# Where sixteen tiles of a rotated context are prepared: twelve in layer 0's attention, four in its feed-forward, none in layer 1's cross attention

## The chip, the cores and the metric

The kernel runs on one core of a Trainium2 chip. The core has five engines that run side by side, each with its own instruction stream: TensorE (PE, matrix products and transposes through them), VectorE (DVE), ScalarE (ACT), GpSimd (POOL) and SyncE (SP, which issues DMA transfers here). They wait for each other through semaphores. The metric is the device time of one execution in microseconds; lower is better.

## The reference

The model is a two-layer perceiver. A latent array `x` of 64 batches with 32 rows of 256 attends to a context `ctx_512` of 64 batches with 257 rows of 64. Each layer is a cross attention, a self attention and a feed-forward, each on a layer norm of `x` and added to `x`:

```python
x = x + _L0_xattn_ref(_layernorm(x), ctx_512, ...)
x = x + _L0_attn_ref(_layernorm(x), ...)      # 16 heads of 128, l2-normed queries and one key head
x = x + _L0_ffn_ref(_layernorm(x), ...)       # 16 blocks of 64; each row uses its 4 likeliest blocks
x = x + _L1_xattn_ref(_layernorm(x), ctx_512, ...)
x = x + _L1_attn_ref(_layernorm(x), ...)      # causal
x = x + _L1_ffn_ref(_layernorm(x), ...)       # 8 experts, one per row
```

The part that matters is the context of layer 1's cross attention, which is rotated by position (rope):

```python
kv_rope = kv_c * cos[None] + _rotate_half(kv_c) * sin[None]
q_r = jnp.einsum('bshq,hqr->bhsr', q_big, W_qr)
k_r = jnp.einsum('bld,hdr->bhlr', kv_rope, W_kr)
attn = jax.nn.softmax(jnp.einsum('bhsr,bhlr->bhsl', q_r, k_r), axis=-1)
ctx_c = jnp.einsum('bhsl,bld->bhsd', attn, kv_rope)
```

`kv_rope` depends on the inputs only, so it can be computed at any time before layer 1. And the feed-forward of layer 0, beside which part of it is now computed:

```python
prob = softmax(xf @ Wr.T + br); _, idx = top_k(prob, 4)      # mask[n, block] = 1 for the four
h = gelu(einsum('nf,ibf->nib', xf, W1b)) * mask[:, :, None]
y = einsum('nib,fib->nf', h, W2b)
```

## The kernel before

The 2048 latent rows are 16 tiles of 128 rows (`NT = 16`), in 4 groups of 4 tiles (`NG = 4`). A context tile `t` is the context of four batches. The stages follow each other in time:

- A (0 to about 130 us): layer 0's cross attention.
- B (130 to 505): layer 0's self attention as a row of slots, one tile entering at each slot `t`. It also holds group 0 of the feed-forward and the block choices of the first groups in its late slots. The order on PE, DVE, ACT and POOL is the order in which the code is written.
- C (505 to 640): groups 1, 2 and 3 of the feed-forward, and small products that fold layer 1's weights (`chain_1`, `chain_2`, `chain_m`, `chain_n`). Only PE's and ACT's order is the written one; a scheduler orders DVE, POOL and SP by its own model of the work.
- D (640 to 990): layer 1's cross attention, 64 blocks `b`, four to a context tile. Then layer 1's self attention and the experts.

**Fetch and rotate.** `fetch(t, work)` (L688) issues ten DMAs on SP: for each half of the tile, the transposed context into `rct` and its two halves swapped into `rrt`; and four pieces of the untransposed context into `rna`. `rotate(t, work)` (L701) runs seven POOL operations on them (two multiplies and an add for the transposed copy, four for the other, L705 to L715), and issues two stores to `ctd` and one to `nad` in DRAM. The tiles `rct`, `rrt`, `rna` and `rnt` have one buffer each, so a fetch waits until the rotation and the stores before it are done with it. Before the change, `rotate(t // 2)` stands at the even slots 0 to 14 of B (tiles 0 to 7) and eight more in D at `b` = 2, 6, ..., 30. Stage D loads `ctd` and `nad` tile by tile.

**The feed-forward.** For each group `g`, `hidden(g, f, ...)` makes eight pieces `hc{g}_{f}` of the hidden layer (matmuls L639, gelu on ACT L646) and multiplies each with its mask `mb[f]` on DVE (L647). The mask of a group is made by `choose_blocks` and `choose_best` (L571 to L615, small DVE operations on 128 x 64 logits: `lgc`, `mxc`, `eqc`, `m2c`, `onec`, `maskc`), written to DRAM as `maskd` (L625) and spread over the partitions by 16 loads (L631, `spread`). `output(g, hs, i, ...)` (L649) then sums the eight pieces for tile `i` into PSUM (`yc`, L652) and adds them to `x` (L659). PE runs, for each `g`, the eight hidden pieces, the choice's logits (`lpc`, for g = 2), the first chains, four outputs with turns between, and the second chains:

```python
chains = {
    (1, 1): [lambda z=z, c=c: chain_1(z, c) for z in range(2) for c in range(2)],
    (2, 0): [lambda z=z: chain_2(z) for z in range(2)],
    (2, 1): [lambda z=z, k=k: chain_m(z, k) for k in range(KC) for z in range(2)],
    (3, 0): [lambda r=r: chain_n(r) for r in range(4)],
}
```

`chain_1` (L1048) multiplies `d_rt` with `d_kr` into `t1`; `chain_2` (L1061) makes `t2` (`d_t2`) out of `t1` and `d_at`; both are copied from PSUM by DVE (L1055, L1068). The weights `d_q`, `d_at`, `d_wo`, `d_kr`, `d_rt`, `d_c` are loaded on SP's queue at the head of C (L1023 to L1035).

**In B**, the steps that the prediction names are: the squares of the queries on POOL (`q2b`, L789), the norm of the projected output (`lnb_bo`, `ynb`), the products with the values (`avb`, L848) and the projection (`yb`, L861). **In D**, a block `b` has the scores (`Sd`, L1345), a softmax with the multiply L1366 and a small one L1368 on DVE, transposes (`pt`, L1382), the product with the context (`od`, L1405), and for every fourth block a projection (`yd`, L1421).

Of the kernel before, what the change touches and what calls it, by code (L numbers as in the profile page):

```python
# [7 lines left out]
F32 = mybir.dt.float32  # L8
# [5 lines left out]
P = 128  # L14
B, S, D = 64, 32, 256
NT = B * S // P
NG = NT // 4
KC = D // P
NKV, DC = 257, 64
NH = 16  # L20
# [25 lines left out]
def perceiver_kernel(ctx: ExitStack, tc: tile.TileContext, a: dict, out: bass.AP):  # L46
    nc = tc.nc
# [16 lines left out]
    def weight(pool, name, shape):  # L64
        return pool.tile(shape, F32, name=name)
# [300 lines left out]
    with tc.tile_pool(name="wA", bufs=2) as work, tc.tile_pool(  # L366
        name="psA", bufs=1, space=PSUM
    ) as ps1, tc.tile_pool(
        name="psA2", bufs=2, space=PSUM
# [312 lines left out]
        tabN.append(tab)  # L682
    cosN, sinN = tabN
    fetched = {}

    def fetch(t, work):

# [33 lines left out]
    with tc.tile_pool(name="wB", bufs=2) as work, tc.tile_pool(  # L721
        name="psB", bufs=1, space=PSUM
# [236 lines left out]
        for t in range(NT + 1):  # L959


            parts = [AHEAD + 4 * t + z for z in range(4)]

            def place(z):
                if z < 4:
                    query_part(parts[z])
                for step in steps.get((t, z), ()):
                    step()

            if t < NT:  # L970
                similar(t)
            place(0)
            if t > 0:
                gather(t - 1)
            if t < NT:
                scale(t)
            place(1)
            square(t + 1)
            ff_late()
            place(2)  # L980
            if t < NT:
                power(t)
            ff_late()
            place(5)
            if t > 0:
                project(t - 1)
                norm_stats(t - 1)
            if t < NT:
                share(t)
            place(3)  # L990
            ff_late()
            if t > 0:
                norm_out(t - 1)
            if t % 2 == 0 and t < NT:
                rotate(t // 2, work)
                if t // 2 + 1 < NT // 2:
                    fetch(t // 2 + 1, work)
            if t == NT - 3:
                rotate_last()
            place(4)  # L1000
            write_pad(t)
            if t in (2, 4):
                load_c(t // 4)
# [12 lines left out]
    with tc.tile_pool(name="wC", bufs=2) as work, tc.tile_pool(  # L1016
        name="psC", bufs=2, space=PSUM
    ) as ps2, tc.manual_schedule(
        engines={mybir.EngineType.PE, mybir.EngineType.Activation}
    ):  # L1020

        d_q = weight(wdp, "d_q", [P, NH, D])
        nc.sync.dma_start(d_q, a["d_wq"].rearrange("(h p) o -> p h o", p=P))  # L1023
# [5 lines left out]
        nc.sync.dma_start(d_kr, a["d_kr"])  # L1029
        d_rt = []  # L1030
        for z in range(2):
            d_rt.append(weight(wdp, f"d_rt{z}", [DC, 8, 192]))
            nc.sync.dma_start(d_rt[z], a["d_rt"][:, 8 * z : 8 * z + 8, :])
        d_c = weight(wdp, "d_c", [P, NH, DC])
        nc.sync.dma_start(d_c, a["d_c"])  # L1035

# [2 lines left out]
        m = w1.tile([P, KC, NH * DC], F32, name="d_m")  # L1039
        n = w1.tile([P, NH // 2, D], F32, name="d_n")  # L1040
        t1 = w1.tile([P, 2, NH, DC], F32, tag="t1", name="d_t1")[0:96]
        t2 = work.tile([P, NH, DC], F32, name="d_t2", bufs=1)
        zs, lkb, lkT = d_q[:, 0:8, :], d_q[:, 8, 0:P], d_q[:, 8, P:D]

        def chain_1(z, c):
            p_ps = ps2.tile([96, 8, DC], F32, tag="w", name=f"t1p{z}_{c}")
            for h in range(8):
                nc.tensor.matmul(  # L1048
                    p_ps[:, h, :],
                    d_rt[z][:, h, c * 96 : (c + 1) * 96],  # L1050
                    d_kr[:, 8 * z + h, :],
                    start=True,
                    stop=True,
                )
            nc.vector.tensor_copy(t1[:, c, 8 * z : 8 * z + 8, :], p_ps)  # L1055
# [99 lines left out]
        def d_context(t, ct, na):  # L1155
# [9 lines left out]
        rot0 = d_context(  # L1165
            0, w1.tile([P, 4, NKV], F32, name="ct_d0"), w1.tile([P, 4, 2, DC], F32, name="na_d0")
        )
        for g in range(1, NG):
            hs = []
            for f in range(8):  # L1170
                hs.append(work.tile([P, 512], F32, tag="h", name=f"hc{g}_{f}", bufs=9))
                hidden(g, f, xT, mb[f], hs[f], ps2, "h")()
            if g == 1:
                mb = spread(2)
                xn = ln_group(2, "c", power=True)
            if g == 2:
                choose_blocks(3, ps2, work)
                choose_best(3, work, range(4))
            if g == 3:
                xn = ln_group(0, "d", power=True)  # L1180
            if g == 3:
                last_load()
            for step in chains.get((g, 0), ()):
                step()
            if g == 3:
                last_turn()
            for i in range(4):
                output(g, hs, i, ps2, "y")
                if (g, i) == (1, 1):
                    xT = transposed(xn, ps2, 2, "c")  # L1190
                    choose_norm(3, act=False)
                if (g, i) == (1, 3):
                    xT_c3 = choose_turn(3, ps2, work)
                if (g, i) == (2, 2):
                    choose_store(3, ps2, work)
                if g == 3 and i == 0:
                    latT[0] = transposed(xn, ps2, 0, "d")
                    queries[0] = w1.tile([P, 8, 8, S], F32, tag="t1", name="qTd0")
                if g == 3:
                    d_queries(0, i, ps2, "w")  # L1200
                    for r2 in ((0, 1), (2, 3), (), ())[i]:
                        last_out(r2)
            if g == 2:
                xT = xT_c3
                mb = spread(3)
            for step in chains.get((g, 1), ()):
                step()
# [4 lines left out]
    with mbw, wd1:  # L1212
# [3 lines left out]
        with tc.tile_pool(name="wD", bufs=2) as work, tc.tile_pool(  # L1216
# [216 lines left out]
            last_keys(0)  # L1433
            score(0)
            rotated(1)
            fetch(NT // 2, work)

            steps, lat = {}, {}
            for g in range(1, NG):
# [22 lines left out]
            for b in range(NB + 2):  # L1462


                if b % 4 == 1 and b // 4 + 2 < NT:
                    rotated(b // 4 + 2)
                if b % 4 == 2 and b // 4 < NT // 2:
                    rotate(b // 4 + NT // 2, work)
                    if b // 4 + 1 < NT // 2:
                        fetch(b // 4 + 1 + NT // 2, work)  # L1470
                if b + 1 < NB:
                    score(b + 1)
                if 1 <= b <= NB:
                    gather(b - 1)
                if b in steps:
                    steps[b]()
                if b % 2 == 0 and b // 8 + 1 < NB // 8:
                    query_part(b // 8 + 1, (b % 8) // 2)
                if b >= 5 and (b - 1) % 4 == 0:
                    project((b - 5) // 4)  # L1480
                if b < NB:
                    turn(b)
                elif b == NB:
                    last_part(NT - 1, ps1.tile([P, 2, 256], F32, tag="o", name="odl"))
                if b == 40:
                    nc.gpsimd.tensor_tensor(e_bk, bc(e_b[:, 1], 2, 2), bc(mask2, 1, KC), ALU.mult)
                if b == 16:

                    e_q = wep.tile([P, KC, D], F32, name="e_q")
                    by_pairs(e_q, a["e_wq"])  # L1490
                    e_k = wep.tile([P, KC, D], F32, name="e_k")
                    for k in range(KC):
                        for z in range(4):
                            o, w = divmod(z, 2)
                            nc.sync.dma_start(
                                e_k[:, k, o * P : (o + 1) * P].rearrange(
                                    "p (r w d) -> p w r d", r=4, w=2
                                )[:, w],
                                a["e_wk"][k * P : (k + 1) * P, :].rearrange(
                                    "p (r d) -> p r d", r=4  # L1500
                                ),
                            )

                    e_b = wep.tile([P, 2, KC], F32, name="e_b")
                    for z, v0 in enumerate((V_BQ, V_BK)):
                        for o in range(KC):
                            for r in range(4):
                                p0 = 64 * (r % 2) + 32 * o
                                nc.sync.dma_start(
                                    e_b[32 * r : 32 * r + 32, z, o : o + 1],  # L1510
                                    a["vecs"][p0 : p0 + 32, v0 + r // 2 : v0 + r // 2 + 1],
                                )
                    e_bk = wep.tile([P, KC, 2], F32, name="e_bk")
                    e_v = wep.tile([P, KC, DC], F32, name="e_v")
                    nc.sync.dma_start(e_v, a["e_wv"].rearrange("(k p) o -> p k o", p=P))
                    f_r = wep.tile([P, KC, 8], F32, name="f_r")
                    nc.sync.dma_start(f_r, a["f_wr"].rearrange("(k p) o -> p k o", p=P))
# [526 lines left out]
```

## Time and profile before

| what | value |
|---|---|
| three runs | 1284.89, 1284.98, 1286.64 us (median 1284.98) |
| the profiled execution, whole / its span | 1285.48 / 1283.7 us |
| mean granted clock of PE | 0.943 |
| PE busy | 1183.7 us, 92% of the span |
| DVE busy | 769.9 us, 60% |
| ACT busy | 555.3 us, 43% |
| POOL busy | 368.2 us, 29% |
| DMA | 103.08 MB, mean 80 GB/s over the span |

The profile is of one execution. Its lines name the source line of the kernel (L705), the engine, the operation and the tiles with their buffer numbers left out. In a timeline a row starts with the time since the start of the span and the duration; rows of like instructions are joined ("x8"), and a bracket at the end tells how long the engine stood before the row and what ended that. PEclk is the clock that PE was granted. A busy share is a mean over stages with different limits; what an edit is worth is read in its own stage.

### The profile page before, as it was taken

To read this page: it belongs to the slowest core of one execution; us is meant where nothing else is said; L and a number is where in the kernel's file an instruction comes from. 1 tells how busy PE (TensorE), PEld (TensorE's weight loads), DVE (VectorE), ACT (ScalarE), POOL (GpSimd) and SP (SyncE) were. 2 spreads that over 40 slices of the span, in tenths; PEclk is the share of its full clock that TensorE was granted. 3 is DMA by queue.
4 is the path that set the end of the run, shared out by engine and by line. 5 is a ranking of instruction groups with operands and counts; after the bars stand their busy time and mean duration, and the time that the engine had idled before them with its cause. 6 is when DMAs were issued, how large, how long until landed. Compare 5 with 4: busy or idle time off the path is not lost. (4 is left out here: it accounts for less than half of the span.)

```text
span 1283.7 us, 26087 instructions
## 1 busy us (share of the span) xinstructions
PE 1183.7 (92%) x10173; PEld 828.5 (65%) x10173; DVE 769.9 (60%) x1801; ACT 555.3 (43%) x1297; POOL 368.2 (29%) x446
## 2 busy tenths in 40 slices
PE   8999999999999998999979999999998797569997
PEld 5656767777676666777757667767765465336664
DVE  5866147778677775433287877776765564434333
ACT  3437344554443641212355646565654454311111
POOL 2433415435451531000154352010011355411111
PEclk8989989999998988979999999999999899669999
DMA  5120123433341423901154354111100434011110
GB/s 151 37 81 21 36 67 94 122 99 108 96 144 44 150 75 103 274 12 68 44 153 105 77 139 110 46 36 47 36 1 2 133 135 163 23 38 42 44 39 18
DMA packets 94971, 103.08 MB, mean 80 GB/s; under 512 B 37792, under 2 KB 71329, under 8 KB 94626
## 3 DMA queue, kind: packets, MB, share of 16 engines
q1 hardware_dynamic: 92978, 97.19, 26.1%
q0 software_dynamic: 1872, 4.23, 0.9%
q8 instruction: 81, 1.33, 0.4%
q14 instruction: 40, 0.33, 0.1%
HBM read 69.45 MB, written 32.85 MB: 80 GB/s over the span
## 5 line engine op out<-in xcount | busy, mean ns | idle before, releaser
L1357 ACT ACTIVATE pp<-Sd,nm 128x257 f32<-128x257 f32 x256 | 118.2, 475 | 75.9 <-DVE nm L1353 71.4
L770 PE MATMUL qb<-xT_b,b_q 128*128 128x256 f32 x512 | 125.3, 394 | 0.0
L770 PEld LDWEIGHTS qb<-xT_b,b_q 128*128 128x128 f32 x512 | 97.4, 195 | 41.4 <-issue 20.9
L861 PE MATMUL yb<-b_o,oTb 128*128 128x256 f32 x512 | 116.4, 386 | 0.0
L861 PEld LDWEIGHTS yb<-b_o,oTb 128*128 128x128 f32 x512 | 98.6, 194 | 14.4 <-issue 1.0
L1366 DVE TENSOR_TENSOR pp<-pp,rd 128x514 f32<-128x514 f32 x128 | 101.1, 790 | 2.1
L1353 DVE TENSOR_REDUCE nm<-Sd 128x2 f32<-128x514 f32 x128 | 82.9, 684 | 19.2 <-PE Sd L1345 19.2
L1388 ACT COPY pTd<-pt 128x512 f32<-128x512 f32 x112 | 61.5, 599 | 52.4 <-PE pt L1382 52.4
L1405 PE MATMUL od<-pTd,na 128*64 128x256 f32 x480 | 66.1, 396 | 11.1 <-issue 9.8
L789 POOL TENSOR_TENSOR q2b<-qTb 128x512 f32<-128x512 f32 x64 | 65.2, 1049 | 28.2 <-ACT qTb L778 18.5
L778 ACT COPY qTb<-qb 128x512 f32<-128x512 f32 x64 | 37.5, 585 | 75.4 <-PE qb L770 73.8
L1345 PE MATMUL Sd<-ct,qTd 64*128 64x257 f32 x480 | 68.8, 404 | 0.6 <-ACT pp L1357 0.6
L880 POOL TENSOR_TENSOR ynb<-ynb,vec 128x256 f32<-128x256 f32 x16 | 11.6, 726 | 194.6 <-DVE ynb L879 194.6
L1382 PE MATMUL pt<-cst,pp 128*128 128x128 f32 x512 | 66.9, 274 | 0.0
L1382 PEld LDWEIGHTS pt<-cst,pp 128*128 128x128 f32 x512 | 58.9, 141 | 9.8 <-issue 5.4
L1143 PE MATMUL qd<-xT_d,d_m 128*128 128x256 f32 x256 | 64.8, 397 | 0.2 <-ACT xT_d L237 0.2
L823 DVE RECIPROCAL rqb<-rqb 128x512 f32<-128x512 f32 x16 | 53.5, 3343 | 17.8 <-ACT rqb L818 17.8
L652 PE MATMUL yc<-c,hc 128*128 128x256 f32 x256 | 61.0, 395 | 2.7 <-DVE hc L647 2.7
L1421 PE MATMUL yd<-d_n,co 128*128 128x256 f32 x256 | 62.0, 397 | 0.0
L1919 POOL DMA_INDIRECT out_dram<-os,ti x23 | 22.7, 985 | 125.0 <-DVE os L1916 103.0
L652 PEld LDWEIGHTS yc<-c,hc 128*128 128x128 f32 x256 | 50.3, 199 | 12.6 <-DVE hc L647 3.5
L1143 PEld LDWEIGHTS qd<-xT_d,d_m 128*128 128x128 f32 x256 | 47.1, 193 | 17.1 <-issue 6.4
(372 smaller groups left out, 2367.6 us busy)
## 6 DMA issues: line engine op xcount, KB each, us to landing
srt<-pad SPq DMA_DIRECT2D x17, 1040.0 KB
mb<-maskd SPq DMA_DIRECT2D x64, 128.0 KB
ct<-ctd SPq DMA_DIRECT2D x30, 257.0 KB
rct<-in_ctxT_dram SPq DMA_DIRECT2D x32, 128.5 KB
rrt<-in_ctxT_dram SPq DMA_DIRECT2D x64, 64.2 KB
ctd<-rct SPq DMA_DIRECT2D x32, 128.5 KB
nad<-rna SPq DMA_DIRECT2D x16, 256.0 KB
fw<-in_f_wg_dram SPq DMA_DIRECT2D x8, 512.0 KB
```

Source lines behind the costliest of these rows:

```text
L652: nc.tensor.matmul(y_ps, hs[f][:, i * P : (i + 1) * P], c_2[:, f, :], start=(f == 0), stop=(f == 7),)
L770: nc.tensor.matmul(q_ps[:, hh, :], b_q[:, k, h * P : (h + 1) * P], xT[:, k, c0 : c0 + 256], start=(k == 0), stop=(k == KC - 1),)
L789: nc.gpsimd.tensor_tensor(q2[:, 4 * h4 : 4 * h4 + 4, :], q, q, ALU.mult)
L861: nc.tensor.matmul(y_ps, oT[:, h, :], b_o[:, h, :], start=(h == 0), stop=(h == NH - 1))
L1143: nc.tensor.matmul(q_ps[:, r, :], m[:, k, pr * P : (pr + 1) * P], xT[:, k, c0 : c0 + 256], start=(k == 0), stop=(k == KC - 1),)
L1345: nc.tensor.matmul(s_ps[:, hh, :NKV], qT[hs, b % 8, 4 * u : 4 * u + 4, :], ct[hs, b % 4, :], start=True, stop=True,)
L1353: nc.vector.tensor_reduce(nm, s_ps[:, :, :NKV], AX.X, ALU.max, negate=True)
L1357: nc.scalar.activation(pp[:, hh, :], s_ps[:, hh, :NKV], AF.Exp, bias=nm[:, hh : hh + 1], accum_out=sd[:, hh : hh + 1],)
L1366: nc.vector.tensor_tensor(pp, pp, bc(rd, 2, NKV), ALU.mult)
L1382: nc.tensor.transpose(pt[:, hh * 256 + u * P : hh * 256 + u * P + P], probs[b][:, u, hh, c * P : (c + 1) * P], ident,)
L1405: nc.tensor.matmul(o_ps[64 * hh : 64 * hh + 64, 0, :], na[:, j, c, :], pT[:, c, hh * 256 : (hh + 1) * 256], start=(c == 0), stop=(c == 1),)
L1421: nc.tensor.matmul(y_ps, co[:, pr, :], n[:, pr, :], start=(pr == 0), stop=False)
```

## The change

Twelve of the sixteen rotations now stand in B, one in each of the slots 0 to 11 (`NR_B = 12`). The tile for slot `t + 1` is fetched right after the rotation at slot `t`. The remaining four stand in C: tile 12 is fetched at the head of C, ahead of layer 1's weights, and `rotate_next` rotates the next tile and fetches the one after at four places, (1, 7), the end of group 1, (2, 3) and (2, 7). D has none left. So that the tiles find room in C, `d_t2` gets no buffer of its own but lies in the memory of `d_rt[0]`, whose tiles get 128 partitions for it. PE's and ACT's instructions and their order are the same as before. DVE's are the same, but between group 2's hidden pieces and its outputs the scheduler orders them otherwise: the eight multiplies `hc2_f * mb`, formerly ahead of nearly the whole choice for group 3, are now spread among the choice's small steps.

```diff
@@ fetch / rotate
     fetched = {}
+    NR_B = 12
@@ stage B, slot t
-            if t % 2 == 0 and t < NT:
-                rotate(t // 2, work)
-                if t // 2 + 1 < NT // 2:
-                    fetch(t // 2 + 1, work)
+            if t < NR_B:
+                rotate(t, work)
+                if t + 1 < NR_B:
+                    fetch(t + 1, work)
@@ head of stage C
+        fetch(NR_B, work)
         d_q = weight(wdp, "d_q", [P, NH, D])
...
-            d_rt.append(weight(wdp, f"d_rt{z}", [DC, 8, 192]))
-            nc.sync.dma_start(d_rt[z], a["d_rt"][:, 8 * z : 8 * z + 8, :])
+            d_rt.append(weight(wdp, f"d_rt{z}", [P, 8, 192]))
+            nc.sync.dma_start(d_rt[z][0:DC], a["d_rt"][:, 8 * z : 8 * z + 8, :])
...
-        t2 = work.tile([P, NH, DC], F32, name="d_t2", bufs=1)
+        t2 = d_rt[0].rearrange("p h q -> p (h q)")[:, 0 : NH * DC].rearrange(
+            "p (h d) -> p h d", h=NH
+        )
...
+        turns = iter(range(NR_B, NT))
+        def rotate_next():
+            t = next(turns, None)
+            if t is not None:
+                rotate(t, work)
+                if t + 1 < NT:
+                    fetch(t + 1, work)
@@ stage C, groups 1 to 3
                 hidden(g, f, xT, mb[f], hs[f], ps2, "h")()
+                if (g, f) in ((1, 7), (2, 3), (2, 7)):
+                    rotate_next()
             if g == 1:
                 mb = spread(2)
...
+            if g == 1:
+                rotate_next()
             if g == 2:
                 xT = xT_c3
                 mb = spread(3)
@@ stage D
             rotated(1)
-            fetch(NT // 2, work)
...
-                if b % 4 == 2 and b // 4 < NT // 2:
-                    rotate(b // 4 + NT // 2, work)
-                    if b // 4 + 1 < NT // 2:
-                        fetch(b // 4 + 1 + NT // 2, work)
```

More of the change, by code (lines that the diff above doesn't have):

```diff
@@ L1049, in chain_1 @@
                     p_ps[:, h, :],
-                    d_rt[z][:, h, c * 96 : (c + 1) * 96],
+                    d_rt[z][0:DC, h, c * 96 : (c + 1) * 96],
                     d_kr[:, 8 * z + h, :],
```

## The prediction

> **What bounds the kernel now.** I read the page first: the span is 1283.7 us, and TensorE (PE) is busy in 92% of it. The 40 slices below, of 32.1 us each, say where it is not. PEclk is the clock that PE was granted, in tenths; POOL is the engine on which every rotation runs.
>
> ```profile
> PE   8999999999999998999979999999998797569997
> PEclk8989989999998988979999999999999899669999
> POOL 2433415435451531000154352010011355411111
> ```
>
> PE sets the pace nearly everywhere, so an edit counts only where it opens or closes a hole on PE. Next, windows by stage. The columns are window, length, busy time of PE, of PE's weight loads, of DVE, ACT and POOL, then clock and DMA. The rows are the feed-forward stage (C), the part of layer 1's cross attention (D) that holds rotations 9 to 15 (rotation 8 starts just ahead of it), and the rest of D, which holds none.
>
> ```profile
> 505.00:640.00 135.00, 134.30 (x605) 98.60 (x603) 50.78 (x145) 34.87 (x56) 4.23 (x5) 0.91 0.37 107
> ...
> 675.00:800.00 125.00, 120.65 (x804) 87.86 (x803) 98.37 (x221) 71.96 (x238) 50.23 (x45) 0.98 0.42 107
> 800.00:990.00 190.00, 184.11 (x1312) 132.39 (x1310) 132.63 (x331) 111.61 (x365) 9.31 (x15) 1.00 0.11 30
> ```
>
> In C PE has 0.7 us of idle time and POOL runs 4.23 us. Work put there meets a full PE, and the only question is whether it delays an operand of PE. The timeline of D shows what a rotation does to the engines beside it:
>
> ```profile
> 663.88 1.58 DVE L1366 TENSOR_TENSOR pp<-pp,rd 128x514 f32<-128x514 f32 x1
> 665.50 1.02 DVE L1368 TENSOR_TENSOR plast<-pp,ones 128x4 f32<-128x4 f32 x1
> ...
> 676.54 0.70 DVE L1366 TENSOR_TENSOR pp<-pp,rd 128x514 f32<-128x514 f32 x1
> 677.27 0.16 DVE L1368 TENSOR_TENSOR plast<-pp,ones 128x4 f32<-128x4 f32 x1
> ...
> 664.87 1.63 POOL L706 TENSOR_TENSOR rrt<-rrt,cst 128x514 f32<-128x514 f32 x1
> ...
> 673.48 1.89 PE L1405 MATMUL od<-pTd,na 128*64 128x256 f32 x8 [3.33 <-issue]
> 675.30 4.56 PE L1421 MATMUL yd<-d_n,co 128*128 128x256 f32 x16
> ...
> 697.11 3.72 PE L1421 MATMUL yd<-d_n,co 128*128 128x256 f32 x16
> ```
>
> During rotation 8 (663.16 to 672.56) a DVE multiply of two SBUF operands takes 1.58 us instead of 0.70, a tiny one 1.02 instead of 0.16. PE then waits 3.33 us, and the next 16 matmuls run at a lower clock: 4.56 us where the same 16 take 3.72 later.
>
> **Removed from D: -8.8 us.** The hole of 3.33 and its 0.84 of slow clock go: 4.2. For the rest I compare strides between projections (yd): from that of tile 1 to that of tile 5 the starts lie 87.51 us apart (697.11 to 784.62), in the next four tiles, without rotations, 82.87 (784.62 to 867.49): 4.64, which holds PE holes of 2.18 and 0.82 at 757 to 761 and a slow projection of 5.41. The gap of 3.15 at 642, which waits on POOL's variance step, stays. -7 to -9.5.
>
> **Four tiles in the feed-forward: what meets them.** SyncE's queue and the DVE order decide:
>
> ```profile
> 508.84 0.38 SPq L1023 DMA_DIRECT2D d_q<-in_d_wq_dram  x1
> ...
> 533.04 0.45 SPq L631 DMA_DIRECT2D mb<-maskd  x1
> ...
> 537.09 7.33 PEld L1048 LDWEIGHTS t1p<-d_kr,d_rt 64*96 64x96 f32 x64 [0.17 <-issue]
> ...
> 561.78 0.68 DVE L647 TENSOR_TENSOR hc<-hc,mb 128x512 f32<-128x512 f32 x1
> 572.71 0.69 DVE L1068 COPY d_t<-t2p 128x512 f32<-128x512 f32 x1 [5.29 <-PE t2p L1061]
> 573.32 0.21 DVE L604 TENSOR_TENSOR eqc<-lgc,mxc 128x64 f32<-128x64 f32 x1
> 578.93 0.42 DVE L659 TENSOR_TENSOR x<-x,yc 128x256 f32<-128x256 f32 x1 [2.30 <-PE yc L652]
> ```
>
> *Late weights, +2.6.* The ten loads of tile 12 are issued ahead of d_q. One fetch occupies the issue queue for 6.7 us (136.04 to 142.74). The mask load at 533.04 waits for the first half of d_rt, so that half landed then; 6.65 later is 539.7, and PE begins chain_1 at 537.09: a stall of 2.6. The second half (534.76, now 541.4) is needed about 543.4, in time. If transfers overlap better it is 0; if the loads share bandwidth, 5.
>
> *DVE order, +4.9.* In before all eight multiplies hc*mb of group 2 are done at 562.4 (the last is shown), ahead of most of group 3's block choice. In the changed kernel the order is interleaved: six multiplies and 22 small steps of the choice stand behind the second t2 copy, which waits for PE until 572.71. Steps go every 0.61 and 0.255 us there, so from 573.3 the last multiply ends 3.7 + 5.6 later, at 582.6. PE needs it for the last two matmuls of group 2's first output, by about 577.7 (that output's add starts at 578.93). So PE stands 4.9. Less if PE already runs late by the 2.6 above? No: the copies move with PE, and the distance stays.
>
> *Clock, +1.9.* Two holes of this size lower the clock as at 673: slow copies of equal work cost 0.84 (4.56 against 3.72), 1.69 (5.41 against 3.72) and, below, 3.05 (10.12 against 7.07). I take the mean of the three, 1.9; 0.8 to 3.1. [...]
>
> *Rotations beside the DVE chain, +7.5.* Following the issue queue: tile 13's loads go after group 2's masks are under way, tile 14's at 566 to 574, so rotation 14 starts about 570 and rotation 15 about 582 to 585, each about 8 us long. They lie over the interleaved chain above, whose steps nearly all have two SBUF operands. A tiny one was stretched from 0.22 to 0.71 and 0.96 in rotating slots at 300 us, or from 0.16 to 1.02 above; a multiply gains 0.9. A whole rotation holds seven POOL operations and lets about one DVE step pass per operation, about 5 us on the chain for one rotation and half of the other, 7.5. It is 0 if neither lands there, 10.5 if both do. [...]
>
> Rotations 12 and 13 (about 548 to 566) meet multiplies with 1.02 us of DVE idle time between them, and the 0.9 that a multiply gains is under that: 0. The d_t2 result in d_rt0's memory waits only for chain_1, done long before: 0. The d_rt tiles with more partitions load the same bytes: 0.
>
> **Four more tiles in layer 0's attention.** Slots 0 to 11 now all rotate. A slot is 18.3 to 23.6 us long. A rotation takes 7.85 us of POOL; in even slots of before, the squares behind it (L789) still end 2.3 to 6.3 us before PE needs them, and by the same arithmetic 2.5 to 5.3 in odd ones. Fetched tiles land 14.7 to 18.1 us after a slot's rotation begins, and the next one needs them 19.8 to 23.5 after it: 0. One odd slot has no room: the choice steps at 317 to 320 now lie under the rotation and squares, so the norm step at 323.69 is about 1.8 late, with 1.25 of slack before the next avb: +0.7 with a little clock (0 to 2).
>
> The last rotation leaves slot 14:
>
> ```profile
> 462.69 2.61 DVE L647 TENSOR_TENSOR hc<-hc,mb 128x512 f32<-128x512 f32 x2
> ...
> 463.68 0.70 PE L652 MATMUL yc<-c,hc 128*128 128x256 f32 x2 [1.70 <-DVE hc L647]
> ...
> 469.62 10.12 PE L861 MATMUL yb<-b_o,oTb 128*128 128x256 f32 x32
> ...
> 493.23 7.07 PE L861 MATMUL yb<-b_o,oTb 128*128 128x256 f32 x32
> ```
>
> A pair of multiplies takes 1.29 at 511; here 2.61 under a rotation, PE stands 1.70 and 0.97, and the clock falls. 1.3 comes back, and of the 3.05 of slow clock I take 0.7: -2.0 (-5.6 to -0.5).
>
> **Sum.** -8.8 + 2.6 + 4.9 + 1.9 + 7.5 + 0.7 - 2.0 = +6.8 on the profiled execution's 1285.48, so 1292.3. That execution lies 0.5 above the median of the runs (1284.98), so 1291.8; I say 1292.
>
> **Rivals.** *Not slower:* rotations 14 and 15 miss the DVE chain, because their transfers land earlier. It decides if rotation 15 is over by 576. Without the 7.5 the sum is -0.7, 1284.3; if slot 14 also keeps its clock (its full -5.6), 1280.7. For it: DMA is 37% busy in C, so transfers need not queue; against: tile 13's loads stand behind the stores of tile 12, and 16 mask loads stand ahead of tile 13's stores. Chance 0.18. *Slower still:* POOL sets the pace of layer 0's attention, because the squares of the six odd slots come 2 us late each: +12 on the sum, about 1304. It decides where a rotation starts over 4 us into the slot; slacks of 2.3 and more in every rotating slot of before speak against it. Chance 0.08. That the change does not do what it says I exclude: its instructions are in the order described. The forecast, slower by a few us: 0.74.
>
> **Range and chances.** The unknown terms, taken at their low ends singly (contention 0, or weights 0 and clock 0.8), reach 1284.3; at their high ends (contention 10.5, weights 5) 1297.2, and a little clock more 1300. The range 1284 to 1300 leaves out under 2 in 10. A measurement of this kernel tells 0.2%, 2.6 us, from no change. Below 1282.4: 0.11; within: 0.14; above 1287.6: 0.75.
>
> **What would show it.** Right: in C, a PE wait of 2 to 3 us before chain_1 and 5 or more before the first yc output of group 2 named after DVE's hc, tiny DVE steps of 0.7 to 1.0 us there, a window of C 15 to 20 us longer; no hole at 673 and tiles 1 to 4 of D at 82.9 per four; slot 14's yc without holes. Wrong: rotations 14 and 15 elsewhere, C longer by under 8 us, or a stretched attention stage with squares as the releaser.

## The result: no difference that the runs can tell

The changed kernel takes 1283.75 us (median of 12 runs, 1278.61 to 1288.74), the kernel before 1284.77 (12 runs beside them, 1277.41 to 1287.25): a ratio of 0.9999, with a 95% interval of 0.9975 to 1.0023 (here and below the ratio comes with its interval and is not the quotient of the two medians, which is 0.9992). The forecast of 1292 is out by 8 us, and the range 1284 to 1300 just misses the time. The three runs known beforehand lay within 1.75 us; with more runs one and the same kernel spreads over about 10.

The profiled execution of the changed kernel takes 1283.49 us, its span 1281.5. First the slices of its page (32.0 us each):

```profile
PE   8999999999999997997989999999999697569997
PEclk8889999999999989977989999999999899669999
POOL 2333327666574302242010000000010355411111
```

Against before, slice 18 of PE (counted from 0; 577 to 609 us, the outputs of group 2) has fallen from 9 tenths to 7, and its clock with it from 9 to 7; slice 15 has gone from 8 to 7. POOL is at 5 to 7 tenths from 192 to 384 us, in the attention, and nearly idle in layer 1's cross attention. The windows by stage say it in numbers (busy times of PE, weight loads, DVE, ACT, POOL, then clock and DMA):

```profile
505.00:640.00 135.00, 121.16 (x537) 86.35 (x538) 53.90 (x118) 32.34 (x52) 35.32 (x30) 0.86 0.48 135
675.00:800.00 125.00, 124.25 (x860) 91.04 (x859) 93.14 (x235) 77.50 (x255) 1.46 (x3) 1.00 0.16 41
```

The feed-forward, full before, now has 13.8 us in which PE stands; the part of layer 1 that held rotations has 0.75 left of 4.35, at full clock. The timeline of the feed-forward shows the losses. In the kernel before, the outputs of group 2 run without a wait:

```profile
572.47 13.34 PE L652 MATMUL yc<-c,hc 128*128 128x256 f32 x48
```

In the changed kernel, PE first, then DVE:

```profile
536.07 8.49 PE L1053 MATMUL t1p<-d_kr,d_rt 64*96 64x64 f32 x64 [1.48 <-DMA d_rt<-in_d_rt_dram]
...
577.44 0.70 PE L652 MATMUL yc<-c,hc 128*128 128x256 f32 x2 [2.11 <-DVE hc L647]
578.95 0.94 PE L652 MATMUL yc<-c,hc 128*128 128x256 f32 x2 [0.81 <-DVE hc L647]
580.72 1.22 PE L652 MATMUL yc<-c,hc 128*128 128x256 f32 x2 [0.83 <-DVE hc L647]
585.28 1.22 PE L652 MATMUL yc<-c,hc 128*128 128x256 f32 x2 [3.34 <-DVE hc L647]
589.77 9.15 PE L652 MATMUL yc<-c,hc 128*128 128x256 f32 x34 [3.27 <-DVE hc L647]
...
575.23 1.30 DVE L605 TENSOR_TENSOR eqc<-eqc,cst 128x64 f32<-128x64 f32 x1
...
588.08 1.64 DVE L647 TENSOR_TENSOR hc<-hc,mb 128x512 f32<-128x512 f32 x1
...
591.02 0.42 DVE L659 TENSOR_TENSOR x<-x,yc 128x256 f32<-128x256 f32 x1 [0.92 <-PE yc L652]
```

Each pair of matmuls waits for a multiply that stands between steps of the choice, and steps that took 0.22 and 0.68 take 1.30 and 1.64 while a rotation runs. And the gains, in slot 14 of the attention and at layer 1's first projection:

```profile
461.25 1.30 PE L652 MATMUL yc<-c,hc 128*128 128x256 f32 x4 [1.44 <-DVE hc L647]
464.89 9.69 PE L862 MATMUL yb<-b_o,oTb 128*128 128x256 f32 x32
...
683.62 1.08 PE L1424 MATMUL od<-pTd,na 128*64 128x256 f32 x8
684.64 3.72 PE L1440 MATMUL yd<-d_n,co 128*128 128x256 f32 x16
```

One hole of 1.44 instead of 1.70 and 0.97; no hole of 3.33 in layer 1, and the projection at full clock (3.72, granted 1.00 from 683.6 to 688.4).

PE's order is the same in both kernels, so the starts of its groups cut the span into pieces that hold the same work on PE in both. Lengths in us, from three profiles of the kernel before and two of the changed one (the repeats are among the experiments below; Sb, yb, t1p, t2p, mp, Sd and yd are PE's groups by their output):

| piece | before | changed | mean difference | forecast |
|---|---|---|---|---|
| start to first yb (A, first slots) | 178.5, 174.5, 176.4 | 180.5, 178.3 | +2.9 | 0 |
| first yb to Sb of slot 12 | 209.39 each | 209.39 each | 0.0 | +0.7 |
| Sb of slot 12 to that of slot 13 | 24.97, 21.89, 21.88 | 21.88, 21.91 | -1.0 | 0 |
| Sb of slot 13 to that of slot 14 | 18.91, 18.92, 18.91 | 18.92, 18.91 | 0.0 | 0 |
| Sb of slot 14 to last yb ("tail") | 61.50, 61.27, 61.10 | 57.44, 55.77 | -4.7 | -2.0 |
| last yb to first t2p ("head") | 68.2, 69.8, 71.1 | 74.0, 73.1 | +3.8 | +2.6, some clock |
| first t2p to first mp ("chain") | 28.1, 29.7, 26.4 | 40.6, 42.4 | +13.5 | +12.4, some clock |
| first mp to first Sd | 51.40 each | 51.40 each | 0.0 | 0 |
| first Sd to last yd (layer 1) | 343.7, 347.2, 345.6 | 333.3, 334.1 | -11.8 | -8.8 |
| last yd to the last ys | 291.2, 291.4, 291.2 | 286.3, 290.6 | -2.9 | 0 |

The sum is -0.2, as are the spans (means 1282.8 and 1282.6); the 7.9 us behind the last ys are equal. Sb of a slot is the first step of that slot in the code. A rotation that the code has at one slot runs on POOL while PE is already in the next (that of slot 11 at 398 us in the changed kernel, PE's slot 12 begins at 390), and the prediction and the expectations name a stretch by the rotation that falls into it: their slot 11 is the piece from Sb of slot 12 to that of slot 13.

### The profile page after: what moved, and what is told of

Read it like the earlier page. It is cut to its first block, busy times and chain, and to the rows that moved or that the text cites. A ratio compares the mean times of both kernels' runs of the same rounds, so it can differ in the third digit from the quotient of the medians.

```text
span 1281.5 us, 26105 instructions
## 1 busy us (share of the span) xinstructions
PE 1179.2 (92%) x10173; PEld 827.1 (65%) x10173; DVE 769.1 (60%) x1801; ACT 555.7 (43%) x1297; POOL 363.9 (28%) x446
## 5 line engine op out<-in xcount | busy, mean ns | idle before, releaser
L1385 DVE TENSOR_TENSOR pp<-pp,rd 128x514 f32<-128x514 f32 x128 | 89.0, 695 | 2.1
L652 PE MATMUL yc<-c,hc 128*128 128x256 f32 x256 | 63.2, 401 | 11.8 <-DVE hc L647 11.8
L790 POOL TENSOR_TENSOR q2b<-qTb 128x512 f32<-128x512 f32 x64 | 65.1, 1046 | 28.2 <-ACT qTb L779 16.9
L1148 PEld LDWEIGHTS qd<-xT_d,d_m 128*128 128x128 f32 x256 | 47.2, 194 | 17.2 <-issue 6.0
L838 DVE RECIPROCAL rdb<-denb 128x512 f32<-128x512 f32 x16 | 53.7, 3355 | 6.3 <-PE denb L836 6.1
```

Of the source, the lines that this page charges most:

```text
L652: nc.tensor.matmul(y_ps, hs[f][:, i * P : (i + 1) * P], c_2[:, f, :], start=(f == 0), stop=(f == 7),)
L790: nc.gpsimd.tensor_tensor(q2[:, 4 * h4 : 4 * h4 + 4, :], q, q, ALU.mult)
L1148: nc.tensor.matmul(q_ps[:, r, :], m[:, k, pr * P : (pr + 1) * P], xT[:, k, c0 : c0 + 256], start=(k == 0), stop=(k == KC - 1),)
L1385: nc.vector.tensor_tensor(pp, pp, bc(rd, 2, NKV), ALU.mult)
```

## The experiments

Theory 1: the change loses in the feed-forward what the prediction said (weights that come late, an interleaved DVE order, contention between DVE and POOL), gains more in attention and layer 1 than it said, and the rest is where slow clock happens to fall. Theory 2: the whole shift of the first two profiles is the change's.

**e1, the attention part alone.** The kernel before, with `NR_B = 12`; in layer 1:

```diff
-                if b % 4 == 2 and b // 4 < NT // 2:
-                    rotate(b // 4 + NT // 2, work)
+                if b % 4 == 2 and b // 4 + NR_B < NT:
+                    rotate(b // 4 + NR_B, work)
```

> Twelve rotations in layer 0's attention, the other four in layer 1's cross attention as before, the feed-forward stage untouched. Theory 1 (holes): the attention stage gains only what its PE holes give, 1.2 us (1.70 + 0.97 before against 1.44 after in slot 14), the rest of its 7.2 us shift in the two profiles is where slow-clock windows happened to fall; of layer 1's 10.4 us the part behind tile 3 comes, 4.8. Sum -6 against before, about 1279. Theory 2 (the whole shift of the attention stage is the change's): -7.2 - 4.8 = -12, about 1273. In the profile: no PE wait in the odd slots 1 to 11 by either.

1272.31 us against 1283.80, ratio 0.9929 (0.9903 to 0.9955): -9.1. That lies between the theories, and the interval, -12.5 to -5.8, holds both; the pieces tell more. The tail is 57.4 us as in the changed kernel, so 4 us of gain there are real and theory 1 had them too small (theory 2 had them too large, by the 3.1 of slot 11 that the repeats below show to be chance); the slots up to 12 stay at 209.41; layer 1 is 340.3, 5.2 under before's mean. No PE wait appears in an odd slot.

**e2, all sixteen in the attention.** As e1 with `NR_B = 16` and no fetch or rotation in layer 1.

> All sixteen rotations in layer 0's attention, one in each slot 0 to 15; none in the feed-forward or in layer 1. Theory 1: layer 1 gains its whole 10.4, slot 14 keeps its hole (0), slots 13 and 15 add 1 to 3 us where multiplies of the feed-forward's group 0 meet a rotation: -8, about 1277. Theory 2 (late slots are what rotations cost most): the four slots 12 to 15 cost 7 more: -3, about 1282.

1267.70 us, ratio 0.9879 (0.9848 to 0.9910): -15.5, twice what theory 1 gave. The tail is 61.3, as before, so rotations in slots 12 to 15 cost no more than those in 12 and 14 did; layer 1 is 332.7, 12.8 under before. The PE rows of slot 14 show both holes again:

```profile
461.02 0.70 PE L652 MATMUL yc<-c,hc 128*128 128x256 f32 x2 [1.68 <-DVE hc L647]
462.69 1.22 PE L652 MATMUL yc<-c,hc 128*128 128x256 f32 x2 [0.97 <-DVE hc L647]
466.98 9.88 PE L862 MATMUL yb<-b_o,oTb 128*128 128x256 f32 x32
```

**e3, DVE in written order in the feed-forward.**

```diff
-        engines={mybir.EngineType.PE, mybir.EngineType.Activation}
+        engines={mybir.EngineType.PE, mybir.EngineType.Activation, mybir.EngineType.DVE}
```

> The changed kernel with DVE of the feed-forward stage in written order too: the eight multiplies of group 2 stand ahead of the whole choice, rotations and loads as in the change. Theory 1 (interleaved order and contention both act through the last multiply): with the multiplies first, neither reaches PE, the 13.2 us between chain_2 and the first mp go, and the time is 11 to 13 under the changed kernel, about 1272. Rival (contention holds DVE whatever the order): about 7.5 stays, 1279.

1276.81 us, ratio 0.9951 (0.9931 to 0.9970). The chain falls to 26.4 us from 41.5, all of its loss; the rotations run as in the change (14 at 564 to 573 us, 15 at 577 to 585). Its PE row, 48 matmuls without a wait, and the place where the gain went:

```profile
570.77 11.84 PE L652 MATMUL yc<-c,hc 128*128 128x256 f32 x48
...
617.54 0.45 PE L1109 MATMUL lkp<-cst,d_q 128*128 128x128 f32 x1 [6.50 <-ACT lns_d L161]
```

In written order the norm statistics for layer 1 stand behind group 3's multiplies, so the piece from mp to Sd is 59.7 instead of 51.4. Theory 1 holds for the chain and missed this. The rival falls: once group 2's multiplies are done, the same rotations cost the chain nothing.

**e4, rotations 14 and 15 out of the chain.** DVE's order between hidden pieces and outputs of group 2 is the changed kernel's.

```diff
-                if (g, f) in ((1, 7), (2, 3), (2, 7)):
+                if (g, f) in ((1, 7), (3, 3), (3, 7)):
```

> The changed kernel with rotations 14 and 15 moved from group 2 into group 3 of the feed-forward; DVE's order between group 2's hidden pieces and outputs is the changed kernel's, word for word. Theory 1: the order's 4.9 to 5.7 stays, the contention's 7.5 goes: mp starts 5 to 6 late instead of 13.2, about 1277 if group 3 hides its rotations. Rival (order alone makes the 13.2): no difference, about 1284.

1278.79 us, ratio 0.9958 (0.9937 to 0.9978). The PE rows of the chain now have small holes:

```profile
568.50 4.06 PE L652 MATMUL yc<-c,hc 128*128 128x256 f32 x8
572.85 1.22 PE L652 MATMUL yc<-c,hc 128*128 128x256 f32 x2 [0.29 <-DVE hc L647]
574.62 1.22 PE L652 MATMUL yc<-c,hc 128*128 128x256 f32 x2 [0.55 <-DVE hc L647]
576.39 1.22 PE L652 MATMUL yc<-c,hc 128*128 128x256 f32 x2 [0.55 <-DVE hc L647]
578.03 8.94 PE L652 MATMUL yc<-c,hc 128*128 128x256 f32 x34 [0.42 <-DVE hc L647]
```

POOL is not in written order in this stage: rotation 14 still ran at 560 to 568, but now ahead of the first yc, and rotation 15 at 605 to 615, behind the chain. From the first yc to the add of the first output it is 6.46 us in before (572.47 to 578.93; 6.42 and 4.86 in its repeats, mean 5.9), 10.78 here (568.50 to 579.28), 18.56 in the changed kernel (572.46 to 591.02; 18.80 in its repeat). So the order costs about 4.9 and the contention 7.9: the prediction had 4.9 and 7.5. But of the order's cost PE stands only 1.8, in four holes; the rest is clock, by the pairs of yc, which take 1.22 here: in the changed kernel's profile such a pair takes 0.70 at a granted clock of 1.00 (577.44) and 1.22 at 0.50 (580.72). The prediction had 4.9 of standing and counted the clock apart. On DVE itself the contention shows without the clock. From the start of the second t2 copy to the end of the last multiply it is 9.2 us here,

```profile
568.75 0.69 DVE L1073 COPY d_rt<-t2p 128x512 f32<-128x512 f32 x1 [4.03 <-PE t2p L1066]
...
577.29 0.68 DVE L647 TENSOR_TENSOR hc<-hc,mb 128x512 f32<-128x512 f32 x1
```

and 17.0 and 17.2 in the two profiles of the changed kernel, with the same steps in the same order: 7.8 and 8.0 more. The whole chain is 34.9 here, 6.8 above before's mean. The rival, order alone, falls.

**e5, e6 and e11, both kernels profiled again**, unchanged.

> The kernel before, profiled a second time, to tell luck from effect. Theory 1: stages that the change does not touch shift by up to 3 us, since slow-clock windows fall elsewhere; the 3.1 us that slot 11 of the attention stage lost in the first profile (qb at 5.84 instead of 3.72 behind the same 2.5 us hole) need not come back, while the slow yb of slot 14 (10.12) and the slow projections of layer 1 do, since their holes are long. Theory 2 (slot 11's loss belongs to the kernel before): it is there again, 3.1.

> The changed kernel, profiled a second time. Theory 1: first mp 13 to 14 us late against group 2's first hidden piece as before, the head of the feed-forward stage 5 late, layer 1 10 to 11 us shorter, no PE wait in slots 0 to 11, each within 1 us of the first profile; only the first stage and the last ones move otherwise.

> The kernel before, profiled a third time, for the spread of its stages: attention tail 61.3 to 61.5, layer 1's cross attention 344 to 347, first mp 28 to 30 us behind chain_2's begin; the time before the first yb anywhere from 174 to 181, and slot 11 either 21.9 or 25.0.

Their pieces are in the table. The slow stretch of slot 11 is gone in both repeats of before, behind the same hole (first profile: 2.09 and 5.84). The second profile:

```profile
390.26 1.14 PE L848 MATMUL avb<-pTb,kvb 32*128 32x512 f32 x8 [2.49 <-DVE pTb L838]
391.33 3.72 PE L770 MATMUL qb<-xT_b,b_q 128*128 128x256 f32 x16
```

It is there in 2 of 13 profiles, once in a kernel with the change's attention (e8), so theory 2 falls for this piece. The untouched start lies between 174.4 and 180.6 in all profiles. The ranges expected for before's chain and tail were too narrow (26.4 and 61.10 came), and the changed kernel's two profiles differ by 1.7 in the tail and 1.8 in the chain, not by under 1. The last piece stays open: 291.2 to 291.4 in before's three profiles, 286.3 to 291.5 in the ten others, with the same code.

**e7, the fetch of tile 12 behind layer 1's weights.**

```diff
-        fetch(NR_B, work)
         d_q = weight(wdp, "d_q", [P, NH, D])
...
         nc.sync.dma_start(d_c, a["d_c"])
+        fetch(NR_B, work)
```

> The changed kernel with the fetch of tile 12 behind the loads of layer 1's weights instead of ahead. DVE's order stays interleaved (the last two multiplies even stand behind the whole choice). Theory 1: no PE wait before chain_1, so the head of the feed-forward stage is 2.5 to 5 us shorter than in the changed kernel; the later chain stays 13 or worse; the time falls by 2 to 4, about 1281. Rival (the head is late for another reason, the store of the masks or the clock): no change there.

1284.22 us, ratio 1.0001 (0.9973 to 1.0030): nothing gained. The DMA wait is gone as theory 1 said, but the head is 73.8, as in the change:

```profile
506.88 12.26 PE L639 MATMUL hp<-xT_c,c 128*128 128x512 f32 x24 [4.13 <-ACT hc L646]
...
539.02 5.38 PE L1052 MATMUL t1p<-d_kr,d_rt 64*96 64x64 f32 x32 [1.46 <-DVE d_t L1059]
```

Rotation 12 now runs from 534 to 543, beside DVE's steps ahead of the t1 copies (three norm steps take 3.70, in before 1.26), and PE waits 1.46 for a copy instead of 1.48 for a load: a wait that took the other's place. The hole of 4.13 ahead of it is no part of the change: e2, which has no rotation there, shows 4.50 and a head of 71.1, and the third profile of before 4.49 and 71.1.

**e8, all four in group 3.** As e7, and:

```diff
-                if (g, f) in ((1, 7), (2, 3), (2, 7)):
+                if (g, f) in ((3, 1), (3, 3), (3, 5), (3, 7)):
...
-            if g == 1:
-                rotate_next()
```

> Twelve rotations in layer 0's attention; the fetch of tile 12 behind layer 1's weights; rotations 12 to 15 all in group 3 of the feed-forward. The scheduler then puts seven of group 2's eight multiplies ahead of the second t2 copy, and the last one too. Theory 1: both losses of the feed-forward go (5 and 13 us), attention keeps 4 to 6 of gain, layer 1 its 10.4; if group 3 hides its rotations, 14 to 16 under the kernel before, about 1269. Rival: group 3's multiplies meet the rotations as group 2's choice did, and 5 to 7 come back: 1275.

1278.07 us, ratio 0.9941 (0.9914 to 0.9967); expected was 1269. Head (69.1) and chain (26.5) are free, as expected, although rotations 12 and 13 did not wait for group 3: they ran at 533 to 541 and 553 to 561 us, 14 and 15 at 586 to 607 and 611 to 619. But mp to Sd takes 64.1 us instead of 51.4, and not by the rival's contention:

```profile
618.82 0.45 PE L1108 MATMUL lkp<-cst,d_q 128*128 128x128 f32 x1 [10.63 <-DMA d_q<-lkd]
```

The profile of SyncE's queue shows why:

```profile
614.95 1.11 SPq L710 DMA_DIRECT2D ctd<-rct  x2
616.10 1.24 SPq L1104 DMA_DIRECT2D d_q<-lkd  x2
```

Two small loads that PE needs stand behind a rotation's stores, and those behind the loads of the tile: they are issued at 616.10, in before at 599.58. The hole of 10.63 and 16 slower matmuls behind it (5.51 instead of 3.62) make up nearly all of the 12.7.

**e9 and e10, no rotation in the feed-forward.** As e1, with other blocks of layer 1 and `NR_B, AT_D = 12, (10, 14, 26, 30)` for e9, `14, (26, 30)` for e10:

```diff
-                if b % 4 == 2 and b // 4 + NR_B < NT:
-                    rotate(b // 4 + NR_B, work)
+                if b in AT_D:
+                    z_ = NR_B + AT_D.index(b)
+                    rotate(z_, work)
```

> Twelve rotations in layer 0's attention, four in layer 1's cross attention at blocks 10, 14, 26 and 30, feed-forward untouched. In the second profile pair only the rotations at block 2 (a hole of 3.3 and a slow projection) and those about blocks 18 and 22 cost layer 1 anything large. Theory 1 (place decides, not number): layer 1 loses about 1 of its 11 to 12, the attention tail keeps its 4 to 5: -15 against before, about 1269. Rival (each rotation in layer 1 costs its share, 1.4): -11, about 1273.

> Fourteen rotations in layer 0's attention (slots 0 to 13), two in layer 1's cross attention at blocks 26 and 30. It tells which late slot costs: by theory 1 the tail's 4 to 5 us belong to the rotation in slot 14 alone, which is not there, so the tail stays at about 56.5 us, layer 1 at 333: -16 against before, about 1268. Rival (every rotation of slots 12 to 14 costs a part): the tail goes back to 59 or 61.

e9: 1272.98 us, ratio 0.9914 (0.9885 to 0.9942), near its rival's 1273, but for another reason. The rotations were not where the code has them, as POOL's rows show (the first operation of the first and second of the four):

```profile
640.95 1.28 POOL L706 TENSOR_TENSOR rct<-rct,cst 128x514 f32<-128x514 f32 x1 [5.88 <-DMA rct<-in_ctxT_dram]
...
657.91 1.28 POOL L706 TENSOR_TENSOR rct<-rct,cst 128x514 f32<-128x514 f32 x1 [8.00 <-DMA rrt<-in_ctxT_dram]
```

Only PE is in written order in layer 1; POOL starts as soon as the tile is there, so "block 10" begins at 641, 8 us behind layer 1's first scores; the four run at 641, 658, 685 and 716, in e1 at 636, 650, 665 and 688. So e9 is close to a second e1, and tells nothing about later blocks. Layer 1 takes 341.1, in e1 340.3, 7.5 to 8.3 over e2's 332.7.

e10: 1265.95 us, ratio 0.9883 (0.9839 to 0.9927): -15, with e2 the fastest of all, no difference between the two. Its two rotations in layer 1 (637 and 680) cost nothing, 332.5; why two cost nothing there and four about 8 is not shown. The tail is 55.2, so the large part of its loss is that of slot 14, as expected; the stretch from Sb of slot 14 to that of 15, though, is 20.8 to 20.9 here as in before and e2, against 19.75 without rotations in slots 12 and 13. The one that all three have is slot 12's: it costs 1.1.

## Why the prediction was wrong

No slowdown came. Over the pieces that the change touches the forecast was +6.8 and the profiles show +0.8. The losses were sized right, and what was foreseen to meet the rotations did meet them; the step that failed is the size of two gains, layer 1's and slot 14's.

- **Feed-forward, 2.6 + 4.9 + 1.9 + 7.5 = 16.9 forecast, 17.3 measured** (3.8 + 13.5). Of the 3.8, 1.6 is not the change's: it lies in group 1's hidden pieces, which take 17.4, 17.3 and 20.3 us from their first matmul to the first yc in before, 20.0 and 19.8 in the changed kernel and 20.3 in e2, which has no rotation there. The weights came late, by less than the 2.6 worked out: DMA waits of 1.48 and 0.73 in the two profiles (2.79 and 1.36 in e3 and e4, which fetch alike), and about 1 of slow clock (t1p takes 8.49 at a mean granted clock of 0.63, in before 7.52 at 0.73). Order and contention are 4.9 and 7.9 by e4, and both act only through the last multiplies, by e3; the order's 4.9 is more clock than standing. The rows show the contention step by step: of the twelve DVE steps that begin beside rotation 15 (580.46 to 589.16, POOL operations of 0.71 to 1.34) six of the choice take 0.51 to 1.30 and not 0.22 to 0.23 as in e4, and a multiply takes 1.64 and not 0.68; with two steps of 1.28 and 1.30 beside the end of rotation 14 that is 7.8 more. The 7.5 of the prediction, worked out from such rows of before, was near it.
- **Layer 1, -8.8 forecast with -9.5 as the far end, -11.8 measured.** The step that failed is the comparison of strides. I took the next four tiles (82.87) as what four tiles cost without rotations; the changed kernel runs tiles 1 to 5 in 81.75 (705.62 to 787.37), and the next four in 82.86, as before. The baseline carried 1.1 of its own: a hole of 1.49 ahead of its last projection, in both kernels, where tiles 1 to 5 end with one of 0.37. One row of before, then two of the changed kernel:

```profile
866.48 1.08 PE L1405 MATMUL od<-pTd,na 128*64 128x256 f32 x8 [1.49 <-issue]
...
786.36 1.08 PE L1424 MATMUL od<-pTd,na 128*64 128x256 f32 x8 [0.37 <-issue]
...
869.22 1.08 PE L1424 MATMUL od<-pTd,na 128*64 128x256 f32 x8 [1.49 <-issue]
```

  The stretch from tile 0 to tile 1 was left out: 0.8 (21.81 against 20.98). The hole at 673 with its clock gave 3.8 of the 4.2 foreseen (34.37 to 30.59 from first Sd to first yd). So against the profile that I read layer 1 is 10.4 shorter (343.7 to 333.3); the other 1.4 comes in because that profile had the shortest layer 1 of three.

- **Slot 14, -2.0 forecast, -4.7 measured** for the tail. The hole was right (2.67 against 1.44). Mis-sized was the clock: I let 0.7 of it come back, but lpc and yc behind the hole (3.43 to 2.67, 1.91 to 1.30), yb (10.12 to 9.69) and the stretch after slot 12's rotation (1.1) all speed up. By e2, which keeps slot 14's rotation and with it the tail of 61.3, and e10, which lacks it and has 55.2, most of this is slot 14's rotation. My own bounds reached to -5.6; I chose the end near the hole.
- **Odd slots, +0.7 forecast, 0.00 measured** in every profile: steps of the choice under a rotation were stretched as foreseen (one at 405 us took 1.31, 0.23 without), but less came of it. The norm step of the slot that I named is 1.3 late and not 1.8 (326.96 against 323.69, in a slot that starts 2.0 later), and the multiply that PE waits for is 1.15 late, inside the 1.25 of slack that I had read.
- **What the runs could tell.** I wrote 0.2%, from three runs within 1.75 us. With 12 runs on each side the interval is 0.24% either way, and one profile differs from another of its kernel by up to 4.3 us in a piece that nobody touched (286.3 and 290.6 behind the last yd).
- The rival "not slower" gave 1284.3, close to the time, by a mechanism that did not happen: rotation 15 ran from 580 to 589, over the chain. Its number was right for a wrong reason. The rival of POOL setting the attention's pace did not come up.

## What to carry to other kernels

Size the work taken away as carefully as the work put in: a row that is stretched and the rows that run at a lower clock behind it (4.56 instead of 3.72 for a projection) belong to the same gain, and the clean stride is best read where exactly the same instructions run undisturbed. Here a rotation was free beside work with slack on DVE and SyncE, not beside an idle POOL: the first twelve cost nothing in the attention's slots (209.39 us in both kernels), where two more cost 8 us beside an interleaved DVE chain (the altered order cost about 5 besides), and 12.7 in a queue ahead of two small loads. On engines that a scheduler orders, the place in the code is not the place in time, so look at the issued order of every queue before pricing a move.

## What the hardware showed that was not expected

The same hole, 2.48 to 2.51 us ahead of avb, costs nothing further in eleven profiles and 3.08 us in two (24.97 against 21.89 from Sb to Sb), with identical code on PE there. For one profile of each kind the place of the hole is set against the clock. In the traces of before (first profile) and of the changed kernel the granted clock is either 1 or 0.5, and its changes are whole multiples of 3.41 us apart. Cut into such steps, counted from the nearest change, the hole has 2.02 us in one step in before, and the clock is 0.5 for the next 6.83 us; in the changed kernel 1.25 and 1.23 us of it fall into two steps, and the clock stays at 1. From the hole on, the mean granted clock is 0.67 in before (391.7 to 402.0) and 1.00 in the changed kernel (393.7 to 404.0), and the 16 matmuls of qb behind it take 5.84 and 3.72. Other profiles and other holes were not compared in this way, so what decides is not shown. The same hole lost PE nothing more in one execution of before and 3.08 us more in another, and a piece is safely compared only over repeated profiles. The first 175 to 181 us, untouched, spread by 6.2 us over the thirteen profiles, more than twice the 2.6 that I took for what a measurement can tell.
